# Gated attention in float32: probabilities transposed on TensorE, or turned in 32x32 blocks on VectorE and moved by DMA

## The chip, the cores and the metric

The kernel runs on one core of one Trainium2 chip. Times are device microseconds of an execution. A profiled execution has its own span, from its first to its last instruction, which is a little shorter than the time that is measured around an execution. The engines are named as in the profile: PE is TensorE (its weight loads apart as PEld), DVE is VectorE, ACT is ScalarE, POOL is GpSimd, and SP is SyncE, whose queue issues all DMAs here.

## The reference, cut to what matters

```python
# x: (4, 512, 256); 16 query heads of 128, 4 key heads
xn = layernorm(x)
Q = (xn @ Wq + bq).reshape(b, l, 16, 128)
K, V = the same with Wk, Wv for 4 heads; head h uses key head h % 4
scores = einsum('blhe,bmhe->bhlm', Q, K) / sqrt(128)
attn = softmax(scores + causal_mask)
ctx = einsum('bhlm,bmhe->blhe', attn, V).reshape(b, l, 2048)
r = xn + gelu(ctx @ Wo + bo)
s = layernorm(r) * gamma + beta
g = silu(swiglu_ffn(xn))          # inner size 1024
return x + s * g
```

All of it is float32. The kernel keeps that accuracy on TensorE by splitting each operand into two parts, hi[...] and lo (the exact rest); `product` (L93) issues three matmuls, hi*hi, hi*lo and lo*hi, on L95, L96 and L97.

## The kernel before, in words

The program has two phases. In the first (up to L589) the tokens of each of the four batches are normed, transposed and put through the feed-forward gate; what the second phase needs of them is written to DRAM (`xT_dram`, `fin_dram`). The second phase is the attention.

The attention works in **groups** (b, g): a batch and a key head with its four query heads. A group has four **steps**, i = 0 to 3, one for each tile of 128 queries; the list `steps` (L560) holds all 64, and the last group goes through its steps in reverse. A step sees i+1 tiles of 128 keys. In the main loop (L632 to L662) each step gives a list of chunks with positions, which are sorted and issued in that order; the framework then schedules the instructions of each engine from that order of priority and the dependences.

For step s the loop issues:

- `scores` (L415) of the next step, in four sub-tiles t of 32 queries of each of the four heads, so that the rows of a sub-tile are (head, query). TensorE makes the scores in a PSUM bank `ps` (two banks); VectorE reduces them with the mask and takes the row minimum (L449); ScalarE does exp with the row sum in `total` (L460); VectorE takes the reciprocal of one column of `total` (L473); GpSimd scales the row (L474). The result stays in one of two tiles `p`, one for each parity of the step's number.
- `transposed_probs` (L476) for each key tile j of step s: four transposes on TensorE against the identity (L481) into a PSUM bank `pt`, which bring (head, query) of the four sub-tiles to columns; then `split_psum` (L82) makes hi on ScalarE (L86) and lo on VectorE (L87). The pairs `pT` live in four slots with the tag "pt".
- `weighted` (L486): pT against the values, accumulated over j in `pc`; at the end `ctxT` is split off it (L89, L90).
- `projected` (L503) of step s-1 with the weights `wos[g]`, and what later steps need: `ahead` (L602) issues `queries` (L401) of the next group, `keys` and `values`.
- now and then the end of the batch before: `activated`, `load_fin`, `finished` (L524 to L544), and the reload of the next batch's transposed tokens (`reload`, L235).

The weights of the projections, `wqs[g]` and `wos[g]`, are loaded and split once by `load_group` (L553) in batch 0 and stay in SBUF for all batches. They take eight of the ten slots of 8 KB per partition with the tag "w"; the other two hold the weights of keys and values.

Of the kernel before, what the change touches and what calls it, by code (L numbers as in the profile page):

```python
# [17 lines left out]
P = 128  # L18
EPS = 1e-5
S = 32  # queries of a head in a tile of scores  # L20
MASK = -1e9
HIGHEST = 3.4028235e38
# [4 lines left out]
def kernel(  # L27
    ctx: ExitStack,
    tc: tile.TileContext,
    x: bass.AP,  # [B, L, D]  # L30
    wq: bass.AP,  # [D, H*E]
    bqT: bass.AP,  # [E, H]
    wk: bass.AP,  # [D, KV*E]
    bkT: bass.AP,  # [E, KV]
    wv: bass.AP,  # [D, KV*E]
    bvT: bass.AP,  # [E, KV]
    wo: bass.AP,  # [H*E, D]
    bo: bass.AP,  # [D]
    gamma: bass.AP,  # [D]
    beta: bass.AP,  # [D]  # L40
    wguT: bass.AP,  # [D, 2*INTER]
    wdT: bass.AP,  # [INTER, D]
    out: bass.AP,  # [B, L, D]
):
# [37 lines left out]
    def split_psum(dst, src, bias=None):  # L82
        """dst[:, 0] = hi, dst[:, 1] = lo of a bank of PSUM (plus a bias per partition)."""
        hi, lo = dst[:, 0], dst[:, 1]
        if bias is None:
            first = nc.scalar.copy(hi, src)  # L86
            second = nc.vector.tensor_tensor(lo, src, hi.bitcast(F32), ALU.subtract)  # L87
        else:
            first = nc.scalar.activation(hi, src, AF.Identity, bias=bias)  # L89
            second = nc.vector.scalar_tensor_tensor(lo, src, bias, hi.bitcast(F32), ALU.add, ALU.subtract)  # L90
        return first, second

    def product(out_ap, lhs, rhs, first, last, **kw):  # L93
        """out += lhs^T rhs; lhs and rhs are (hi, lo)."""
# [19 lines left out]
    def load_w(name, views, hi_on=None, lo_on=None):  # L114
        """A slot of 1024 columns of weights, in two parts."""
# [17 lines left out]
    # Probabilities of a query tile: [32 queries of each head of a group, sub-tile of 32  # L133
    # queries, keys], the last key that the tile sees in the last column. What a sub-tile
    # doesn't see of the last P keys stays zero.
    p_tiles = [const.tile([P, NT, L], F32, name=f"p{k}") for k in range(2)]

# [18 lines left out]
    # The first tokens and the first weights come in small pieces, in the order of their use.  # L156
# [14 lines left out]
    def split_first(f, lo_on=None):  # L171
        """The columns of f of the first slot of the gate's weights."""
# [8 lines left out]
    # Keeps the tensor engine busy until the first tokens are there, so that its clock is up by then.  # L181
# [114 lines left out]
    ff_tags = [("s", 2), ("s", 2), ("t", 2), ("t", 2), ("mm", 1), ("c", 1)]  # L296
    def h_tiles(b):
        """Places for the eight tiles of a batch among those of the attention phase."""
# [4 lines left out]
        else:  # L303
            yield from (pair("k", 4, f"hk_{b}_{k}") for k in range(4))
        if b % 2:
            yield from (pair("v", 5, f"hv_{b}_{k}") for k in range(4))
# [57 lines left out]
    banks = ["mm", "c"]  # "c" only until the first values are weighted  # L364
# [5 lines left out]
    def whole(dst, t):  # L370
        """The first P columns as they were before they were split: so few columns go
        faster through the tensor engine whole."""
        nc.gpsimd.tensor_tensor(dst, t[:, 0].bitcast(F32), t[:, 1].bitcast(F32), ALU.add)  # L373

    def keys(b, g):
# [4 lines left out]
        k = pair("k", 4, f"kT_{b}_{g}")  # L380
# [20 lines left out]
    def queries(b, g, r):  # L401
        h = r * KV + g
        pq = psum.tile([P, L], F32, tag=free_bank(), bufs=1, name=f"pq_{b}_{h}")
        w = wqs[g]
# [3 lines left out]
        if r == 0:  # L408
            # [E, part, sub-tile of S queries, head of g, query]
# [6 lines left out]
    def scores(b, g, i, t):  # L416
        """Causal scores of sub-tile t of query tile i, of the four heads of g, as
        probabilities. Kept negated up to exp, so that the minimum of a row is the bias
        that exp wants."""
# [53 lines left out]
        latest["dve"] = [nc.vector.reciprocal(total[:, r : r + 1], total[:, r : r + 1])]  # L473
        latest["pool"] = [nc.gpsimd.tensor_scalar(pr, pr, total[:, r : r + 1], 1.0, ALU.mult, ALU.mult)]  # L474
# [11 lines left out]
    def weighted(b, g, i, j):  # L486
        """Transposed probabilities against the values: [E, heads of g, queries of i]."""
# [17 lines left out]
    def projected(b, g, i, r):  # L505
        first = g == 0 and r == 0 and i < 2
        if first:
# [6 lines left out]
            (wos[g][:, 0, ts(r, D)], wos[g][:, 1, ts(r, D)]),  # L514
# [19 lines left out]
    def finished(b, t, last):  # L534
        """Residual, second layer norm, gate and the outer residual of token tile t."""
# [23 lines left out]
    load_group(0)  # L559
# [8 lines left out]
    for b in range(B):  # L568
        for f in range(NI):
# [14 lines left out]
            elif f == 6:  # L584
                values(0, 0)
            else:
                keys(0, 1)
    for t in range(NT):
        down(B - 1, t)  # L589
    for p in p_tiles:  # L590
        clear(p, L)
    for r in range(G):
        scores(0, 0, 0, r)
        if r > 1:
            keys(0, r)
    values(0, 1)
    banks = ["mm"]
    load_group(1)

    # ---- attention: scores run one step ahead of the weighted values, queries one  # L600
    # group, the projection one step behind ----
    def ahead(b, g, n):  # L602
        """What later steps need."""
        if g == 0 and n + 1 < NT and (b, n) != (0, 0):
            yield values, (b, n + 1)
        dist = TUNE.get("qd", (1, 1, 1, 1))
        mine = range(sum(dist[:n]), sum(dist[: n + 1]))
        if g + 1 < KV:
            for r in mine:
                yield queries, (b, g + 1, r)  # L610
        elif b + 1 < B:
            if n == 0:
                reload(b + 1)
            yield keys, (b + 1, n)
            for r in mine:
                yield queries, (b + 1, 0, r)
            if n == NT - 1:
                yield values, (b + 1, 0)

    def load_group_behind(g, half):  # L620
        with behind("pool"):
            load_group(g, half)
# [9 lines left out]
    for s, (b, g, i) in enumerate(steps[:-2]):  # L632
        n = s % NT
        chunks = []
        for m, (f, a) in enumerate(ahead(b, g, n)):
            # The scores of the next group follow its last queries.
            pos = TUNE.get("a0", 0.01) + TUNE.get("a1", 0.3) * m
            chunks.append((min(pos, -1.0) if f is queries and n == NT - 1 else pos, f, a))
        for r in range(G):
            if s + 4 < len(steps):  # L640
                chunks.append((TUNE.get("s0", 0.05) + TUNE.get("s1", 0.17) * r, scores, steps[s + 1] + (r,)))
            elif s + 4 == len(steps):
                for m in range(1, 4):
                    chunks.append((TUNE.get("l0", 0.05) + TUNE.get("l1", 0.17) * r + TUNE.get("l2", 0.1) * m, scores, steps[s + m] + (r,)))
# [14 lines left out]
        if b == 0 and g + 2 < KV and n in (1, 2):  # L659
            chunks.append((0.9, load_group_behind, (g + 2, n - 1)))  # L660
# [3 lines left out]
    # The last two steps run side by side.  # L664
# [84 lines left out]
```

## Time and profile before

| | |
|---|---|
| time, median of 3 runs (lowest, highest) | 681.08 us (680.22, 681.22) |
| span of the profiled execution | 679.5 us |
| mean granted TensorE clock | 0.994 |
| DMA, mean over the span | 51 GB/s; SP's queue 15.4% of 16 engines |
| bytes moved | 34.73 MB |
| L474, scaling on POOL | x256, mean 505 ns, 127.6 us busy |
| L460, exp on ACT | x256, mean 522 ns, 133.2 us busy |
| L87, lo of pT on DVE | x160, mean 686 ns, 106.6 us busy |
| L86, hi of pT on ACT | x160, mean 587 ns, 89.2 us busy |
| L473, reciprocal on DVE | x256, mean 158 ns, 38.4 us busy |

The span and every duration are those of one profiled execution. "Busy" is the time in which an engine had an instruction in work; matmuls overlap in their pipeline, so that the durations of single matmuls add up to more than TensorE's time. A row of the group table names the line, the engine, the operation, what it writes and reads, the shape, the count, the busy time with the mean of one in ns, and the idle time of the engine just before with what ended it. The chain of waits goes back from the last instruction to whatever released it.

### The profile page before, as it was taken

How to read it: one execution, taken by the hardware profiler on the slowest of the kernel's cores; microseconds unless marked ns; L12 is line 12 of the kernel's file. 1: busy time of each engine (PE TensorE's matmuls, PEld its weight loads, DVE VectorE, ACT ScalarE, POOL GpSimd, SP SyncE). 2: the span in 40 equal slices, each digit the busy share in tenths (PEclk: the TensorE clock that was granted, in tenths of full speed). 3: DMA queues.
4: the chain of work that ended last, by engine and by line, in shares of the span. 5: the costliest groups of instructions: out<-in, count | busy, mean ns of one | idle time of the engine just before them, and what ended most of it. 6: DMA issues, size and time to landing. Idle time of an engine off the chain costs nothing.

```text
span 679.5 us, 12006 instructions
## 1 busy us (share of the span) xinstructions
PE 661.7 (97%) x3996; PEld 581.6 (86%) x3996; DVE 447.8 (66%) x1337; ACT 402.6 (59%) x956; POOL 273.4 (40%) x490
## 2 busy tenths in 40 slices
PE   7979999999999999999999999999999999999995
PEld 6768888889889888888888898889888988888984
DVE  5864434165766766775787666668867766687867
ACT  4434333253765766677676665957666668576772
POOL 5588130720646423222353232216433323354332
PEclk8999999999999999999999999999999999999998
DMA  7753322211310100000022000002210000032000
GB/s 223 246 191 122 127 81 90 77 47 50 92 31 2 36 29 1 1 0 1 20 76 94 1 0 1 2 1 63 63 62 1 1 2 1 1 93 79 1 1 32
DMA packets 25262, 34.73 MB, mean 51 GB/s; under 512 B 2288, under 2 KB 18544, under 8 KB 25200
## 3 DMA queue, kind: packets, MB, share of 16 engines
q1 hardware_dynamic: 25200, 33.97, 15.4%
q8 instruction: 31, 0.51, 0.3%
q14 instruction: 31, 0.25, 0.1%
HBM read 21.38 MB, written 12.58 MB: 50 GB/s over the span
## 4 chain that ended last, share of the span: by engine, by line
PE 89%; DVE 4%; DMA 4%; issue 1%; ACT 1%; POOL 1%; SPq 0%; ACTq 0%; DVEq 0%; POOLq 0%
PE pt L481 10%; PE pc L96 5%; PE pc L95 5%; PE pc L97 5%; PE pq L95 5%; PE py L97 4%; PE ps L97 4%; PE ps L96 4%; PE pq L97 4%; PE pq L96 4%; PE py L95 4%; PE ps L95 4%; PE py L96 4%; PE pg L97 3%; PE pg L96 3%; PE pg L95 3%
## 5 line engine op out<-in xcount | busy, mean ns | idle before, releaser
L474 POOL TENSOR_SCALAR p<-p,total 128x320 f32<-128x320 f32 (+15 forms) x256 | 127.6, 505 | 195.5 <-DVE total L473 174.9
L460 ACT ACTIVATE p<-p,least 128x320 f32<-128x320 f32 (+15 forms) x256 | 133.2, 522 | 59.7 <-DVE least L449 51.0
L449 DVE CUSTOM_DVE_ANT_0 p<-ps,mask 128x320 f32<-128x320 f32 (+15 forms) x256 | 109.8, 435 | 42.6 <-PE ps L97 17.5
L86 ACT CAST pT<-pt 128x512 fp32r<-128x512 f32 x160 | 89.2, 587 | 60.0 <-PE pt L481 59.2
L87 DVE TENSOR_TENSOR pT<-pt,pT 128x512 fp32r<-128x512 f32 x160 | 106.6, 686 | 25.5 <-ACT pT L86 25.0
L481 PE MATMUL pt<-ident,p 128*128 128x128 f32 x640 | 107.2, 273 | 0.5 <-POOL p L474 0.5
L481 PEld LDWEIGHTS pt<-ident,p 128*128 128x128 f32 x640 | 81.1, 142 | 17.5 <-POOL p L474 0.7
L97 PE MATMUL py<-w_o,ctxT 128*128 128x256 f32 x256 | 73.5, 287 | 0.6 <-DVE ctxT L90 0.6
L95 PE MATMUL py<-w_o,ctxT 128*128 128x256 f32 x256 | 72.9, 285 | 0.1
L96 PE MATMUL py<-w_o,ctxT 128*128 128x256 f32 x256 | 72.1, 281 | 0.0
L96 PE MATMUL pc<-pT,v 128*128 128x512 f32 x160 | 69.1, 432 | 0.0
L95 PE MATMUL ps<-kT,qT 128*128 128x288 f32 (+3 forms) x192 | 68.5, 357 | 0.0
L373 POOL TENSOR_TENSOR q<-qT 128x128 f32<-128x128 f32 x64 | 30.4, 474 | 93.7 <-DVE qT L90 55.8
L95 PE MATMUL pc<-pT,v 128*128 128x512 f32 x160 | 64.5, 403 | 0.1
L97 PE MATMUL pc<-pT,v 128*128 128x512 f32 x160 | 63.2, 395 | 0.0
L473 DVE RECIPROCAL total<-total 128x1 f32<-128x1 f32 x256 | 38.4, 158 | 37.2 <-ACT p L460 35.1
L96 PE MATMUL ps<-kT,qT 128*128 128x288 f32 (+3 forms) x192 | 62.2, 324 | 0.0
L97 PE MATMUL ps<-kT,qT 128*128 128x288 f32 (+3 forms) x192 | 61.7, 322 | 0.0
L90 DVE SCALAR_TENSOR_TENSOR qT<-pq,bq_sb,qT 128x512 fp32r<-128x512 f32 x64 | 47.9, 748 | 15.3 <-ACT qT L89 15.3
L89 ACT ACTIVATE qT<-pq,bq_sb 128x512 fp32r<-128x512 f32 x64 | 44.0, 687 | 20.1 <-PE pq L97 19.6
L90 DVE SCALAR_TENSOR_TENSOR ctxT<-pc,bv_sb,ctxT 128x512 fp32r<-128x512 f32 x64 | 47.8, 747 | 11.1 <-ACT ctxT L89 10.5
L95 PE MATMUL pg<-xT,w_gu 128*128 128x512 f32 (+1 forms) x132 | 50.5, 397 | 3.9 <-DVE h L338 2.5
(127 smaller groups left out, 1567.5 us busy)
## 6 DMA issues: line engine op xcount, KB each, us to landing
fin<-fin_dram SPq DMA_DIRECT2D x16, 384.0 KB, 3.2
xT_dram<-xT SPq DMA_DIRECT2D x8, 512.0 KB, 2.6
fin_dram<-gate SPq DMA_DIRECT2D x16, 256.0 KB, 2.0
xT_again<-xT_dram SPq DMA_DIRECT2D x8, 512.0 KB, 3.9
fin_dram<-xn SPq DMA_DIRECT2D x16, 128.0 KB, 2.4
st_q<-in_wq_dram SPq DMA_DIRECT2D x8, 256.0 KB, 3.2
st_o<-in_wo_dram SPq DMA_DIRECT2D x4, 512.0 KB, 3.9
out_dram<-y SPq DMA_DIRECT2D x16, 128.0 KB, 1.7
```

Source lines behind the costliest of these rows:

```text
L86: first = nc.scalar.copy(hi, src)
L87: second = nc.vector.tensor_tensor(lo, src, hi.bitcast(F32), ALU.subtract)
L89: first = nc.scalar.activation(hi, src, AF.Identity, bias=bias)
L90: second = nc.vector.scalar_tensor_tensor(lo, src, bias, hi.bitcast(F32), ALU.add, ALU.subtract)
L95: nc.tensor.matmul(out_ap, lhs[0], rhs[0], start=first, stop=False, **kw)
L96: nc.tensor.matmul(out_ap, lhs[0], rhs[1], start=False, stop=False, **kw)
L97: nc.tensor.matmul(out_ap, lhs[1], rhs[0], start=False, stop=last, **kw)
L449: nc.vector.tensor_tensor_reduce(pr, ps[:, :seen], mask[:, L - seen :], scale=-SCALE, scalar=HIGHEST, op0=ALU.add, op1=ALU.min, accum_out= ...
L460: exp = nc.scalar.activation(pr, pr, AF.Exp, bias=least[:, r : r + 1], scale=-1.0, accum_out=total[:, r : r + 1],)
L473: latest["dve"] = [nc.vector.reciprocal(total[:, r : r + 1], total[:, r : r + 1])]
L474: latest["pool"] = [nc.gpsimd.tensor_scalar(pr, pr, total[:, r : r + 1], 1.0, ALU.mult, ALU.mult)]
L481: nc.tensor.transpose(pt[:, :, t], p[:, t, ts(j, P)], ident)
```

## The change

For the steps that `moved` names (i > 0, and not one of the last three), the probabilities no longer go through TensorE to be transposed:

- The reciprocal is taken once for a step, of all four columns of `total`, behind the fourth exp. The four scalings on GpSimd follow it (`normalized`).
- VectorE turns each scaled sub-tile in blocks of 32x32 (`nc.vector.transpose`) into a tile `pu` in a "w" slot.
- `exchanged` writes `pu` to DRAM in one DMA, and reads it back in four DMAs, each of which lands in 32 partitions, into `pw` in another "w" slot. The blocks are then where the transposes would have put them.
- `transposed_probs` splits `pw`: hi on ScalarE, lo on VectorE for even j and on GpSimd for odd j, both from SBUF.

Scores run three steps ahead (`AHEAD`). Steps i = 0 have two tiles of their own for the probabilities (`p_first`), and are transposed on TensorE as before. Because `pu` and `pw` use "w" slots, the weights of the projections don't stay: their split form is written to DRAM in batch 0 (`w_dram`) and loaded for each later group. Keys are made two groups ahead in three slots in place of four; queries of the next groups, the reload of xT and the loads of weights move to other steps.

```diff
+AHEAD = 3
...
+    p_first = [const.tile([P, NT, P], F32, name=f"pf{k}") for k in range(2)]
...
+    w_dram = {(k, g): dram.tile([P, 2, 1024], F32, tag=f"w{k}{g}", name=f"w_dram_{k}{g}") for k in "qo" for g in range(KV)}
...
-        k = pair("k", 4, f"kT_{b}_{g}")
+        k = pair("k", 3, f"kT_{b}_{g}")
...
+            elif i == 0:
+                p = p_first[(b * KV + g) % 2]
             else:
                 p = p_tiles[steps.index((b, g, i)) % 2][:, :, L - n :]
...
-        latest["dve"] = [nc.vector.reciprocal(total[:, r : r + 1], total[:, r : r + 1])]
-        latest["pool"] = [nc.gpsimd.tensor_scalar(pr, pr, total[:, r : r + 1], 1.0, ALU.mult, ALU.mult)]
+        if t == G - 1:
+            latest["dve"] = [nc.vector.reciprocal(total, total)]
+            for k in range(NT):
+                normalized(b, g, i, k)
+
+    def normalized(b, g, i, t):
+        p, _, total = probs[b, g, i]
+        pr = p[:, t, : i * P + (t + 1) * S]
+        latest["pool"] = [nc.gpsimd.tensor_scalar(pr, pr, total[:, t : t + 1], 1.0, ALU.mult, ALU.mult)]
+        if moved(b, g, i):
+            if t == 0:
+                turned[b, g, i] = work.tile([P, NT, i + 1, NT, S], F32, tag="w", bufs=10, name=f"pu_{b}_{g}_{i}")
+            u = turned[b, g, i]
+            nc.vector.transpose(u[:, :, :, t], p[:, t].rearrange("p (j c k) -> p c j k", c=NT, k=S))
+
+    def moved(b, g, i):
+        return i > 0 and (b, g, i) not in steps[-3:]
+
+    def exchanged(b, g, i):
+        u = turned.pop((b, g, i)).rearrange("p c j t n -> p (c j t n)")
+        n = (i + 1) * P
+        d = dram.tile([G, S, NT, n], F32, tag="pd", bufs=3, name=f"pd_{b}_{g}_{i}")
+        nc.sync.dma_start(d.rearrange("r k c n -> (r k) (c n)"), u)
+        w = work.tile([P, G, n], F32, tag="w", bufs=10, name=f"pw_{b}_{g}_{i}")
+        for c in range(NT):
+            nc.sync.dma_start(w[ts(c, S)], d[:, :, c].rearrange("r k n -> k r n"))
+        placed[b, g, i] = w
 
     def transposed_probs(b, g, i, j):
+        if moved(b, g, i):
+            src = placed[b, g, i][:, :, ts(j, P)]
+            t = pair("pt", 4, f"pT_{b}_{g}_{i}_{j}")
+            hi, lo = (t[:, k].rearrange("p (r n) -> p r n", r=G) for k in range(2))
+            nc.scalar.copy(hi, src)
+            (nc.gpsimd if j % 2 else nc.vector).tensor_tensor(lo, src, hi.bitcast(F32), ALU.subtract)
+            pT[b, g, i, j] = t
+            return
...
-    def load_group(g, half=None):
-        if half != 1:
-            wqs[g] = load_w(f"q{g}", [wq_v[c, g] for c in range(ND)])
-        if half != 0:
-            wos[g] = load_w(f"o{g}", [wo_v[g]])
+    def load_group(kind, ph):
+        b, g = divmod(ph, KV)
+        to = wqs if kind == "q" else wos
+        if b == 0:
+            views = [wq_v[c, g] for c in range(ND)] if kind == "q" else [wo_v[g]]
+            to[ph] = load_w(f"{kind}{g}", views)
+            nc.sync.dma_start(w_dram[kind, g], to[ph].bitcast(F32))
+        else:
+            to[ph] = work.tile([P, 2, 1024], F32R, tag="w", bufs=10, name=f"w_{kind}_{b}_{g}")
+            nc.sync.dma_start(to[ph].bitcast(F32), w_dram[kind, g])
...
+    for i in range(1, AHEAD):
+        for r in range(G):
+            scores(0, 0, i, r)
+            if i == AHEAD - 1 and r % 2:
+                queries(0, 1, r // 2)
+        exchanged(0, 0, i)
...
+        ph = b * KV + g
+        if n == NT - 1:
+            if ph + 2 < B * KV:
+                yield keys, divmod(ph + 2, KV)
+                for r in range(2):
+                    yield queries, (*divmod(ph + 2, KV), r)
+        if n == 0 and ph + 1 < B * KV:
+            for r in range(2, G):
+                yield queries, (*divmod(ph + 1, KV), r)
...
+        if s + AHEAD < len(steps):
+            step = steps[s + AHEAD]
+            for r in range(G):
+                chunks.append((TUNE["s0"] + TUNE["s1"] * r, scores, step + (r,)))
+            if moved(*step):
+                chunks.append((1.9, exchanged, step))
...
+        if n == 1 and ph + 1 < B * KV:
+            chunks.append((0.9, load_group_behind, ("o", ph + 1)))
+        if n == 0 and ph + 2 < B * KV:
+            chunks.append((0.9, load_group_behind, ("q", ph + 2)))
+        if n == 1 and g == KV - 2 and b + 1 < B:
+            chunks.append((0.9, reload, (b + 1,)))
```

More of the change, by code (lines that the diff above doesn't have):

```diff
@@ L303, in h_tiles @@
         else:
-            yield from (pair("k", 4, f"hk_{b}_{k}") for k in range(4))
+            yield from (pair("k", 3, f"hk_{b}_{k}") for k in range(3))
         if b % 2:
-            yield from (pair("v", 5, f"hv_{b}_{k}") for k in range(4))
+            yield from (pair("v", 5, f"hv_{b}_{k}") for k in range(5))
     n_ff = 0
@@ L403, in queries @@
         pq = psum.tile([P, L], F32, tag=free_bank(), bufs=1, name=f"pq_{b}_{h}")
-        w = wqs[g]
+        w = wqs[b * KV + g]
         for c in range(ND):
@@ L513, in projected @@
             (c[:, 0, ts(r, P)], c[:, 1, ts(r, P)]),
-            (wos[g][:, 0, ts(r, D)], wos[g][:, 1, ts(r, D)]),
+            (wos[b * KV + g][:, 0, ts(r, D)], wos[b * KV + g][:, 1, ts(r, D)]),
             first,
@@ L551 @@
     wv_sb = load_w("v", [wv.rearrange("(c p) n -> p c n", p=P)])
-    def load_group(g, half=None):
-        if half != 1:
-            wqs[g] = load_w(f"q{g}", [wq_v[c, g] for c in range(ND)])
-        if half != 0:
-            wos[g] = load_w(f"o{g}", [wo_v[g]])
-    load_group(0)
+    def load_group(kind, ph):
[8 more added lines that the diff above has]
+            nc.sync.dma_start(to[ph].bitcast(F32), w_dram[kind, g])
+    load_group("q", 0)
+    load_group("o", 0)
     steps = []
@@ L587 @@
                 keys(0, 1)
+    placed, turned = {}, {}
     for t in range(NT):
@@ L591 @@
         clear(p, L)
+    for p in p_first:
+        clear(p, P)
+    load_group("q", 1)
     for r in range(G):
         scores(0, 0, 0, r)
-        if r > 1:
-            keys(0, r)
     values(0, 1)
     banks = ["mm"]
-    load_group(1)
+    for i in range(1, AHEAD):
[4 more added lines that the diff above has]
+        exchanged(0, 0, i)
     def ahead(b, g, n):
@@ L605, in ahead, with load_group_behind @@
             yield values, (b, n + 1)
[L606 to L622, printed above, removed]
+        ph = b * KV + g
[7 more added lines that the diff above has]
+                yield queries, (*divmod(ph + 1, KV), r)
+        if g == KV - 1 and b + 1 < B and n == NT - 1:
+            yield values, (b + 1, 0)
+    def load_group_behind(kind, ph):
+        with behind("pool") if ph < KV else nullcontext():
+            load_group(kind, ph)
     def finished_behind(b, t):
@@ L637 @@
             pos = TUNE.get("a0", 0.01) + TUNE.get("a1", 0.3) * m
[L638 to L644, printed above, removed]
+            chunks.append((pos, f, a))
+        if s + AHEAD < len(steps):
[4 more added lines that the diff above has]
+                chunks.append((1.9, exchanged, step))
         for j in range(i + 1):
@@ L658 @@
                 chunks.append((TUNE.get("fin_pos", 0.7), finished_behind, (b - 1, n)))
-        if b == 0 and g + 2 < KV and n in (1, 2):
-            chunks.append((0.9, load_group_behind, (g + 2, n - 1)))
+        ph = b * KV + g
+        if n == 1 and ph + 1 < B * KV:
[4 more added lines that the diff above has]
+            chunks.append((0.9, reload, (b + 1,)))
         for _, f, a in sorted(chunks, key=lambda c: c[0]):
```

## The prediction

> **What bounds the kernel now.** I read the busy table and the chain of waits first, then windows of one batch, then the rows of the operations that the change touches.
>
> ```profile
> PE 661.7 (97%) x3996; PEld 581.6 (86%) x3996; DVE 447.8 (66%) x1337; ACT 402.6 (59%) x956; POOL 273.4 (40%) x490
> ...
> PE pt L481 10%; PE pc L96 5%; PE pc L95 5%; PE pc L97 5%; PE pq L95 5%; PE py L97 4%; PE ps L97 4%; PE ps L96 4%; PE pq L97 4%; PE pq L96 4%; PE py L95 4%; PE ps L95 4%; PE py L96 4%; PE pg L97 3%; PE pg L96 3%; PE pg L95 3%
> ...
> L481 PE MATMUL pt<-ident,p 128*128 128x128 f32 x640 | 107.2, 273 | 0.5 <-POOL p L474 0.5
> ```
>
> TensorE is busy 97% of the span, and nearly every link of the chain is a TensorE product that waits for nothing. The transposes of L481 are the chain's largest line. Their row overstates them: 273 ns is a pipelined duration. The chain in order of time, in one stretch, has the real price:
>
> ```profile
> 307.57 0.19 PE ps L97
> 307.76 0.44 PE pt L481 x4
> 308.20 0.24 PE pq L95
> 308.44 0.23 PE pq L96
> ```
>
> Four transposes hold TensorE for 0.44 us, so one costs 0.11 us (and a product of 512 columns 0.23 us). Next, the batch between two reloads of xT, then the early stretch in which the DMA engines were saturated:
>
> ```profile
> 363.44:493.00 129.56, 129.16 (x796) 114.14 (x795) 91.77 (x298) 87.44 (x213) 46.18 (x92) 1.00 0.08 26
> ```
> ```profile
> 44.00:48.00 4.00, 4.00 (x21) 3.34 (x20) 0.69 (x1) 0.61 (x2) 1.64 (x2) 1.00 1.04 349
> ```
>
> After the length come busy us of TensorE, its weight loads, VectorE, ScalarE and GpSimd, then granted clock, DMA share and GB/s. A batch has 4 groups (b, g), so a group takes 32.4 us, with VectorE busy 22.9, ScalarE 21.9 and GpSimd 11.5; DMA is nearly idle (0.08). The second line gives the DMA ceiling: about 349 GB/s.
>
> **TensorE: what goes.** A group has steps i = 0 to 3, step i with i+1 key tiles of four transposes. Steps i > 0 hold 4 x (2+3+4) = 36. All 16 groups: 576, less the last three steps' 12+8 = 20: 556. At 0.11 us: **61.2 us** off the path, 4.0 us a group, leaving 28.4. (The chain's 10% of 679.5 us, times 556/640, says 59.) No matmul is added.
>
> **The engines that take over.** VectorE gains twelve 32x32 transposes a group. No row shows one. Nearest are its passes over as many elements: L449 takes 0.55 us for 384 columns and 0.68 for 512; by these 4 x (0.42+0.55+0.68) = 6.6 us; at twice that,[...] 13.2; below 6.6 nothing in the trace points. I take 6.6. One reciprocal replaces four: 12 x 0.158 = 1.9 less. Nine differences from PSUM at 0.686 = 6.2 go; five from SBUF come back. L343, two SBUF inputs, takes 0.74 to 1.05 us, and 0.68 is the lowest such row (L112 on VectorE): 3.4 to 5.2. Sum 24.8 to 26.6 of 28.4. GpSimd gets the other four differences: L112 there takes 1.35 us, 5.4 more: 17 of 28.4. ScalarE's copies read SBUF (L342, 0.62) in place of PSUM (0.587): 22.2. None of the three exceeds 28.4; with the dear transposes VectorE would need 31 to 33, about the present pace.
>
> **DMA.** Per group each moved step writes and reads 512, 768 or 1024 KB: 2.36 MB each way. The weights no longer stay in place (two loads of 1 MB a group; in batch 0 a write of 1 MB beside each of wq and wo's own first load, 3.1 MB). Reloads of xT, fin and out are 0.8 MB as before. Sum 7.6 MB, at 349 GB/s **21.8 us of 28.4**: it fits, but the queue goes from 8% to three quarters full.
>
> **The wait that is added.** A step's probabilities now make a round trip: scores, exp, scaling, turning, write, read, split, weighted product. Landing times:
>
> ```profile
> xT_dram<-xT SPq DMA_DIRECT2D x8, 512.0 KB, 2.6
> fin_dram<-gate SPq DMA_DIRECT2D x16, 256.0 KB, 2.0
> xT_again<-xT_dram SPq DMA_DIRECT2D x8, 512.0 KB, 3.9
> ...
> out_dram<-y SPq DMA_DIRECT2D x16, 128.0 KB, 1.7
> ```
>
> 128, 256 and 512 KB written land after 1.7, 2.0 and 2.6 us: 1.4 us plus 0.3 per 128 KB. The write takes 2.6, 3.2 and 3.8 us for i = 1, 2, 3. Reads: the reload's shortest landing is 3.2 us for 512 KB, which leaves about 2.0 fixed. By these rows a read takes 3.2, 3.8 and 4.4 us.
>
> [...] Each exchange reads in four DMAs that land in 32 partitions each (32c to 32c+31); every large transfer of this trace spans 128.[...] The data part then doubles: 4.4, 5.6 and 6.8 us. By the row the queue holds 21.8 us a group[...]. No row of before decides it[...].
>
> Before the write, the tail of a step of 512 columns shows the chain up to the scaling:
>
> ```profile
> 317.47 0.40 PE L97 MATMUL ps<-kT,qT 128*128 128x512 f32 x1
> 318.02 0.69 DVE L449 CUSTOM_DVE_ANT_0 p<-ps,mask 128x512 f32<-128x512 f32 x1 [0.66 <-PE pt L481]
> 318.89 0.73 ACT L460 ACTIVATE p<-p,least 128x512 f32<-128x512 f32 x1
> 319.74 0.16 DVE L473 RECIPROCAL total<-total 128x1 f32<-128x1 f32 x1
> 320.07 0.70 POOL L474 TENSOR_SCALAR p<-p,total 128x512 f32<-128x512 f32 x1 [2.01 <-DVE total L473]
> ```
>
> From the product's end (317.87) to the start of scaling (320.07) is 2.2 us. Now one reciprocal serves four sub-tiles, so four scalings start together: 0.62+0.67+0.70+0.70 = 2.7, then the last transpose 0.7: 5.6 us. Write 3.8, SP's issue 0.35 (0.34 per DMA in the queue's timeline), read 6.8, copy 0.62 and difference 0.68 to 1.35 (1.0): **18.2 us for i = 3 with nothing in the way**; 15.8 by the row. For i = 2: 4.9+3.2+0.35+5.6+1.6 = 15.7 (13.9).
>
> Against this stands TensorE's work between the last score of a step and its first weighted product in the changed program's order, counted at the rates above: medians of 16.2 us for i = 1, 14.3 for i = 2, 16.9 for i = 3. That is all the cover "three ahead" gives. What is in the way: SP is in order, each read waits there for its write to land, and the next write, weights, fin and out stand behind it. In most groups the 1 MB load of wq stands before the write of i = 3: 1.05 MB/349 = 3.0 us. Engine queues add about 0.5 (the 448-column pair before the tail above took 3.8 us where the tail took 2.9). So i = 3 needs 18.2+3.5 = 21.7 against 16.9, a stall of **4.8 us a group**; i = 2 needs 15.7+1.0 = 16.7 against 14.3, which mostly falls into the same stall; I add 0.5. Break-even is 4.0.
>
> **Sum against the profiled execution.** 15.4 groups (556/36): 679.5 - 61.2 + 15.4 x 5.3 = 699.9 us; with the 1.6 us by which the median (681.08) exceeds the span: **702 us**, 3% slower. Edits at nothing: GpSimd's two clears of p_first and the three smaller reciprocals of i = 0 (GpSimd is 60% idle; uncovered under 1 us); loads of weights moved a group later (wq stands half a group before its first query; if late, 3 us once a group, as in the upper rival). The first phase, some 170 us, and the last three steps are unchanged.
>
> **Rivals.** (1) *Faster: reads run as the reload's row.* Then i = 3 needs 15.8+3.0 = 18.8, a stall of 1.9: 679.5-61.2+29.3+1.6 = **649**. For it: the only reads in the trace, and DMA at 8%. Against: the landing shape. It decides wherever the stall stays under 4.0 us a group. (2) *Much slower: the late landing feeds itself.* In the new VectorE order the difference of step 1 (it waits for its read) stands before the transposes of step 3, and that of step 3 before the next group's. So VectorE closes a loop: exchange 1 (2.6+0.35+4.4 = 7.4), difference 0.7, two reductions, exp, scaling, turning 5.5, exchange 3 (11.0), difference 0.7, the next group's 4: 29.3, and with wq ahead 32.3 before any other queueing. Behind a waiting difference also stand the reductions that empty the two score banks, so TensorE stops in one piece.[...] this trace shows 1.00 in every stretch of the attention, 0.91 only in its first 20 us. By the row such stalls cost their length[...]. With both: stalls of 8 us, 679.5-61.2+123+1.6 = **743**.[...] (3) *Even:* gain and stalls cancel, 4.0 each, **681**. That the change doesn't do what it says: the new order has 84 transposes left of 640, so no.
>
> **Chances.** 702: 0.40; 649: 0.32; 743: 0.20; 681: 0.08. The likeliest's own range is 686 to 722 (queueing of 2.5 to 4.8). Range **640 to 755**. A difference of 0.2% is what this measurement can tell: faster 0.35 (rival 1 and 0.03 of the even case), same 0.04, slower 0.61.
>
> **What would show it.** Right: L481 with 84 instructions; TensorE's idle grown to about 80 us, before weighted products whose differences wait for pw; DMA share near 0.7 in the attention; the read's landing clearly above 4.4 us for i = 3. Wrong: landings of 4.4 or less with TensorE busy over 95% (rival 1); granted clock under 1.00 in mid-attention (rival 2); transposes at 1.3 us for 512 columns would make VectorE the bound.

## The result, and the profile after

The changed kernel takes **765.92 us** at the median (764.16 to 773.1, 4 runs) against 681.15 us before (680.22 to 682.73): a ratio of 1.126, 95% interval 1.1226 to 1.1294. The direction of the forecast holds; its size does not, 85 us slower in place of 21. The profiled execution is one of 773.1 us with a span of 771.0, 91.5 us above the span of before, and all accounts below are of such single executions.

From the profile of the changed kernel: busy times, the chain by engine, five rows of the group table (line, engine, operation, what it writes and reads, count, busy us and mean ns, then the idle time ahead of it and what ended it), and DMA issues (KB each, median us to landing).

```profile
PE 659.5 (86%) x3440; PEld 552.7 (72%) x3440; DVE 499.0 (65%) x1267; ACT 397.4 (52%) x956; POOL 359.7 (47%) x558
...
PE 35%; DMA 32%; DVE 14%; ACT 7%; SPq 5%; issue 4%; POOL 2%; ACTq 0%; DVEq 0%; POOLq 0%
...
L520 POOL TENSOR_TENSOR pT<-pw,pT 128x512 fp32r<-128x512 f32 x62 | 84.4, 1368 | 167.7 <-ACT pT L519 153.3
...
L519 ACT CAST pT<-pw 128x512 fp32r<-128x512 f32 x139 | 77.7, 615 | 104.4 <-DMA pw<-pd 101.0
...
L520 DVE TENSOR_TENSOR pT<-pw,pT 128x512 fp32r<-128x512 f32 x77 | 74.1, 965 | 70.4 <-ACT pT L519 70.4
L96 PE MATMUL pc<-pT,v 128*128 128x512 f32 x160 | 73.3, 458 | 48.8 <-ACT pT L519 48.1
...
L495 DVE STREAM_TRANSPOSE pu<-p 128x256 f32<-128x256 f32 (+2 forms) x184 | 94.9, 555 | 2.1 <-POOL p L488 1.9
...
pd<-pu SPq DMA_DIRECT2D x16, 1024.0 KB, 6.8
pw<-pd SPq DMA_DIRECT2D x64, 256.0 KB, 5.3
...
pw<-pd SPq DMA_DIRECT2D x60, 192.0 KB, 3.9
...
pw<-pd SPq DMA_DIRECT2D x60, 128.0 KB, 2.8
```

556 matmuls are gone (3996 to 3440), but TensorE's busy time fell by 2 us only. So the remaining ones became slower, and on top TensorE is idle for 111 us of the span where it was idle for 18. The chain, nearly all TensorE before, is one third DMA. The wait runs down a line of engines: the read ends ScalarE's idle time (L519, 101.0 us), and ScalarE's hi part (the cast to fp32r) ends that of VectorE and GpSimd (L520) and TensorE's ahead of weighted products (48.1 us), which begin with hi. The batch between two reloads of xT took 129.6 us before; it is now

```profile
395.17:541.40 146.23, 124.73 (x646) 104.14 (x646) 103.54 (x270) 84.18 (x208) 67.31 (x106) 0.94 0.63 200
```

with a granted clock of 0.94 in place of 1.00 and a DMA share of 0.63 in place of 0.08 (columns as in the forecast). The clock is the first thing that the forecast's sum did not have.

To see what the pieces are worth I added up TensorE's time from the last product of the first phase to the end, counting for each matmul the time from its start to the next one's start (its own duration at most), and the gaps between as idle:

| us, one execution each | span | transposes | idle | all other products |
|---|---|---|---|---|
| before | 679.5 | 54.4 | 2.3 | 447.8 |
| after | 771.0 | 7.7 | 95.6 | 491.3 |
| difference | +91.5 | -46.7 | +93.3 | +43.5 |

The three differences sum to 90.1; the first phase and the tail bring 1.4. Most of the 43.5 us is work at half clock: between the first and the last product of the attention the trace grants half speed for 85.3 us, against none before. TensorE stands idle for 16 of these. In the other 69 a product of 512 columns starts 0.43 us after the one before at the median, against 0.23 at full clock; this and the granted 0.50 put the loss at 34 us, an estimate. The remaining 9.5 us lie at full clock, in products just ahead of a gap: the sum counts a product of 512 columns there with its own 0.4 us, where the next would have started after 0.23. They belong to the waits.

Two stretches of the after trace, each a window of 3.41 us and the next one (length, then busy us of TensorE, its weight loads, VectorE, ScalarE and GpSimd, then granted clock, DMA share, GB/s):

```profile
369.49:372.90 3.41, 1.89 (x11) 1.45 (x10) 1.89 (x8) 1.79 (x4) 0.58 (x1) 1.00 1.07 378
372.90:376.31 3.41, 3.41 (x10) 2.44 (x9) 3.25 (x10) 1.55 (x7) 1.86 (x3) 0.50 0.96 380
```
```profile
441.19:444.60 3.41, 0.33 (x3) 0.30 (x2) 1.99 (x8) 2.61 (x7) 1.39 (x2) 1.00 1.00 411
444.60:448.01 3.41, 3.41 (x11) 2.77 (x10) 1.31 (x4) 0.37 (x2) 1.99 (x5) 0.50 0.32 130
```

In each pair TensorE is idle for a part of the first window and then works through the second at half speed, 10 and 11 products where the full-speed window from 448.01 holds 21. In the first pair 1.52 us of idle came ahead of the half clock.

### The profile page after: what moved, and what is told of

It reads as the page before. It is cut to its first block, busy times and chain, and to the rows that moved or that the text cites. A ratio compares the mean times of both kernels' runs of the same rounds, so it can differ in the third digit from the quotient of the medians.

```text
span 771.0 us, 11159 instructions
## 1 busy us (share of the span) xinstructions
PE 659.5 (86%) x3440; PEld 552.7 (72%) x3440; DVE 499.0 (65%) x1267; ACT 397.4 (52%) x956; POOL 359.7 (47%) x558
## 4 chain that ended last, share of the span: by engine, by line
PE 35%; DMA 32%; DVE 14%; ACT 7%; SPq 5%; issue 4%; POOL 2%; ACTq 0%; DVEq 0%; POOLq 0%
DMA pw<-pd 18%; DMA pd<-pu 13%; DVE pu L495 5%; SPq L511 5%; PE pg L97 4%; PE pg L96 4%; PE pg L98 4%; ACT pT L519 3%; PE pc L96 3%; PE pc L97 2%; PE pd L96 2%; PE pc L98 2%; PE pd L98 2%; PE pd L97 2%; DVE p L456 2%
## 5 line engine op out<-in xcount | busy, mean ns | idle before, releaser
L520 POOL TENSOR_TENSOR pT<-pw,pT 128x512 fp32r<-128x512 f32 x62 | 84.4, 1368 | 167.7 <-ACT pT L519 153.3
L467 ACT ACTIVATE p<-p,least 128x160 f32<-128x160 f32 (+3 forms) x196 | 111.1, 568 | 45.7 <-DVE least L456 37.7
L519 ACT CAST pT<-pw 128x512 fp32r<-128x512 f32 x139 | 77.7, 615 | 104.4 <-DMA pw<-pd 101.0
L488 POOL TENSOR_SCALAR p<-p,total 128x160 f32<-128x160 f32 (+3 forms) x196 | 105.4, 559 | 43.7 <-DVE total L481 35.8
L520 DVE TENSOR_TENSOR pT<-pw,pT 128x512 fp32r<-128x512 f32 x77 | 74.1, 965 | 70.4 <-ACT pT L519 70.4
L96 PE MATMUL pc<-pT,v 128*128 128x512 f32 x160 | 73.3, 458 | 48.8 <-ACT pT L519 48.1
L456 DVE CUSTOM_DVE_ANT_0 p<-ps,mask 128x160 f32<-128x160 f32 (+3 forms) x196 | 94.0, 487 | 28.9 <-PE ps L98 27.8
L495 DVE STREAM_TRANSPOSE pu<-p 128x256 f32<-128x256 f32 (+2 forms) x184 | 94.9, 555 | 2.1 <-POOL p L488 1.9
L97 PE MATMUL pc<-pT,v 128*128 128x512 f32 x160 | 71.1, 444 | 5.4 <-POOL pT L520 3.5
L96 PE MATMUL ps<-kT,qT 128*128 128x160 f32 (+2 forms) x192 | 66.2, 345 | 2.1 <-DVE least L456 1.8
L96 PE MATMUL pq<-xT_again,w_q 128*128 128x512 f32 x128 | 56.1, 438 | 12.6 <-DVE qT L91 7.8
L97 PE MATMUL ps<-kT,qT 128*128 128x160 f32 (+2 forms) x192 | 64.1, 334 | 0.0
L98 PE MATMUL ps<-kT,qT 128*128 128x160 f32 (+2 forms) x192 | 63.8, 332 | 0.0
L96 PEld LDWEIGHTS py<-w_o,ctxT 128*128 128x128 f32 x256 | 49.4, 193 | 17.8 <-ACT ctxT L90 15.0
```

What stands on the lines that cost most here:

```text
L96: nc.tensor.matmul(out_ap, lhs[0], rhs[0], start=first, stop=False, **kw)
L97: nc.tensor.matmul(out_ap, lhs[0], rhs[1], start=False, stop=False, **kw)
L98: nc.tensor.matmul(out_ap, lhs[1], rhs[0], start=False, stop=last, **kw)
L456: nc.vector.tensor_tensor_reduce(pr, ps[:, :seen], mask[:, L - seen :], scale=-SCALE, scalar=HIGHEST, op0=ALU.add, op1=ALU.min, accum_out= ...
L467: exp = nc.scalar.activation(pr, pr, AF.Exp, bias=least[:, r : r + 1], scale=-1.0, accum_out=total[:, r : r + 1],)
L488: latest["pool"] = [nc.gpsimd.tensor_scalar(pr, pr, total[:, t : t + 1], 1.0, ALU.mult, ALU.mult)]
```

## The experiments

All ratios are against the kernel before on the same chip, with their 95% intervals. "Exchange" means the DMA write and its four reads; "turning" the 32x32 transposes on VectorE.

**What does the exchange cost, what VectorE's load, what the rearrangement?** Three kernels take the change apart. In the first the splits take `pu` itself, so that no block changes its partitions; in the second GpSimd's scaling writes `pu` as well, and VectorE turns nothing; the third moves no step, keeps the three steps of lookahead and the reloaded weights, and gives the probabilities "w" slots of their own.

```diff
 def exchanged(b, g, i):                       # e1, e5
-    nc.sync.dma_start(d..., u)
-    for c in range(NT): nc.sync.dma_start(w[ts(c, S)], d[:, :, c]...)
+    w = u.rearrange("p (r n) -> p r n", n=n)
 def normalized(b, g, i, t):                   # e5
-    tensor_scalar(pr, pr, ...); nc.vector.transpose(u[:, :, :, t], ...)
+    nc.gpsimd.tensor_scalar(flat[:, t], p[:, t], ...)
 def moved(b, g, i):                           # e8
-    return i > 0 and (b, g, i) not in steps[-3:]
+    return False
```

> The write to DRAM and the reads back are left out: the splits take the turned blocks as they lie in SBUF, so blocks stand in the wrong places of the output; all else stays, the reloaded weights too. If the loss sits in the round trip through DRAM (its landing times and what waits behind them), TensorE is the bound again: 620 to 645 us, clock 0.99. If the added work on VectorE, GpSimd and ScalarE or the reloaded weights cost it, 690 us or more remain.

> As the run without the exchange (680 us), and the turning is left out too: GpSimd's scaling writes the tile that the splits read, over all columns, so blocks stand unturned. VectorE loses 184 instructions, some 95 us of work. If VectorE's load is what ate the gain in the run without the exchange, the time falls to 635 to 655 us. If it is GpSimd, ScalarE, the reloaded weights or the new order of queries and keys, it stays at 670 to 685.

> No step is moved: all probabilities go through TensorE as before, in tiles of their own; scores still run three steps ahead, weights are still written to DRAM and reloaded, reciprocals are merged, queries and keys stand where the change put them. If the rearrangement and the reloaded weights are harmless, 680 to 688 us; if they cost by themselves, 695 us or more.

Measured: e1 679.8 us, 0.9983 [0.9963, 1.0003]; e5 648.76 us, 0.9521 [0.9505, 0.9537]; e8 682.67 us, 1.0015 [1.0006, 1.0024]. So the rearrangement costs nearly nothing, and with turning and exchange both gone the removed transposes bring 34 us. The turning takes 31 us of that back although it issues nothing on TensorE. The exchange costs the other 86 us. The surprise was e1: I had expected 620 to 645 us. The window 360 to 480 us, first of e1, then of e5:

```profile
360.00:480.00 120.00, 113.48 (x632) 97.13 (x631) 104.68 (x268) 83.13 (x203) 68.20 (x105) 1.00 0.26 93
```
```profile
360.00:480.00 120.00, 115.05 (x650) 99.62 (x649) 83.75 (x233) 86.30 (x212) 71.53 (x109) 1.00 0.27 97
```

In e1 VectorE is busy 104.68 of 120 us, 87%, in e5 70%, with the clock at 1.00 in both windows. An engine at 87% is not full, and yet TensorE loses: by the sum above its idle time is 38.2 us in e1 and 20.3 in e5, and over the whole attention e1 runs 13.7 us at half clock, e5 none. The longest such wait, VectorE's queue in e1 first, then TensorE's:

```profile
208.17 4.22 DVE L516 TENSOR_TENSOR pT<-pu,pT 128x512 fp32r<-128x512 f32 x1
...
212.89 0.74 DVE L91 SCALAR_TENSOR_TENSOR ctxT<-pc,bv_sb,ctxT 128x512 fp32r<-128x512 f32 x1
```
```profile
213.68 0.39 PE L98 MATMUL py<-w_o,ctxT 128*128 128x256 f32 x1 [3.92 <-DVE ctxT L91]
```

The instruction that TensorE waits for stands behind a difference that took 4.22 us, where the mean of its line in e1 is 1.15, and behind one reduction. Waits for this line sum to 10.1 us in e1 and 2.6 in e5. Such long differences are not the turning's own: e5 has one of 4.28 us at the same place, and TensorE waits 1.49 us there. That the turning makes VectorE's queue longer is seen; how its 31 us divide among the waits was not followed further.

**Is the exchange's cost the wait as such, or its volume?** e12 keeps every write and its four reads, but of 64 columns.

```diff
-        d = dram.tile([G, S, NT, n], F32, tag="pd", ...)
-        nc.sync.dma_start(d.rearrange("r k c n -> (r k) (c n)"), u)
+        d = dram.tile([P, 64], F32, tag="pd", ...)
+        nc.sync.dma_start(d, u[:, :64])
         for c in range(NT):
-            nc.sync.dma_start(w[ts(c, S)], d[:, :, c].rearrange("r k n -> k r n"))
+            nc.sync.dma_start(u[ts(c, S), :64], d[ts(c, S)])
```

> The changed kernel with each exchange kept as a round trip, but of 64 of the columns only (32 KB written, four reads of 8 KB back into the same tile); the splits take the tile. Left out: the move of the blocks between partitions. Without an exchange the kernel took 680 us, with the full one 766 us. If what the exchange costs is the volume (transfers of 0.5 to 1 MB at some 200 to 400 GB/s, and what they put in each other's way), a small round trip of about 4 us is nearly covered: 680 to 700 us. If it is that any wait for a DMA in the order of the engines stalls TensorE, most of the 86 us stays: 735 us or more. Between them, the share of each is read off: at 710 us, 30 us belong to the wait itself and 56 us to the volume.

Measured: 679.34 us, 0.9968 [0.995, 0.9986], the same as with no exchange. ScalarE's row of e12, and two rows of its DMA issues:

```profile
L519 ACT CAST pT<-pu 128x512 fp32r<-128x512 f32 x139 | 79.0, 616 | 14.2 <-DMA pu<-pd 10.7
```
```profile
pu<-pd SPq DMA_DIRECT2D x184, 8.0 KB, 1.6
...
pd<-pu SPq DMA_DIRECT2D x46, 32.0 KB, 1.5
```

A round trip of 1.5 + 1.6 us is covered (10.7 us of waiting, not 101.0). The 86 us go with the volume, 0.5 to 1 MB each way, and with what waits behind such transfers. e1, e5 and e12 also take no slot for `pw`; but in the changed kernel the turning does not wait for a slot there (2.1 us of idle ahead of L495, ended by the scaling), and SP's queue shows no wait of note for one.

**Does VectorE's load still count when the exchange is there?** e11 is e5's scaling with the full exchange.

> The changed kernel with the exchange as it is, but without the turning on VectorE: GpSimd's scaling writes the tile that is written to DRAM. Left out: the transposition inside the 32x32 blocks. Without the exchange, the turning cost 31 us (680 against 649 us). If load and exchange add up, this kernel takes about 735 us. If the wait for the round trip hides VectorE's load, since turning adds only 0.7 us to a trip of 24 us, it takes 755 to 766 us. If VectorE's load lengthens every trip by queueing, it gains more than 31 us: under 725 us.

Measured: 740.07 us, 1.0831 [1.0773, 1.0889]. Against 766 us the turning costs 26 us here by the medians, 29 by the ratios, and 31 us without an exchange: the two costs nearly add.

**What makes the volume so dear: the shape in which the reads land, the order of VectorE's queue, the load of wq?** e2 reads into all 128 partitions in each of the four DMAs. e4 issues the splits of a step only behind the next moved step's last turning, scaling and exp, so that no waiting split stands ahead of them. e13 is both, e10 is e4 with the 1 MB load of wq behind the reads of i = 3.

```diff
-            nc.sync.dma_start(w[ts(c, S)], d[:, :, c].rearrange("r k n -> k r n"))    # e2, e13
+            nc.sync.dma_start(w[:, c], d[:, :, c].rearrange("r k n -> (r k) n"))
...
+            with ExitStack() as stack:                                                 # e4, e10, e13
+                for ins in last.get(steps[nxt], []):
+                    stack.enter_context(tc.issue_after(ins.ins))
                 nc.scalar.copy(hi, src)
```

> The four reads of a step each land in 128 partitions with n columns in place of 32 partitions with 4n: same bytes, same packet length, same count, but the heads and key blocks are not exchanged, so the output is not the reference's. [...] the read of 1 MB gets some 2.4 us shorter and the time falls to 690 to 725 us. If reads are bound by packets or by DRAM, landings stay (5.3 us at 1 MB) and the time stays at 755 to 775.

> The splits of a moved step are queued behind the next moved step's turning (VectorE), scaling (GpSimd) and last exp (ScalarE), so that no engine holds the next exchange back while it waits for a landing. Nothing else changes. If the late landing feeds itself through VectorE's and GpSimd's order, the loop opens: 695 to 735 us. If each step's own round trip is longer than its cover, the order is no matter: 755 to 775 us.

> e2_reads_128 and e4_order in one: reads into 128 partitions (750 us alone) and the splits queued behind the next exchanged step's turning and exp (738 us alone); the changed kernel is at 766 us. Left out: the blocks land in the wrong partitions. If the two add up, 722 us. If both shorten the same wait in the loop of exchange and VectorE's order, the second is worth less: 730 to 738 us. If the shorter reads, with the loop cut, bring the trip under the cover, it falls below 710 us.

> As e4_order (738 us), with the 1 MB load of wq queued behind the four reads of i = 3 in place of ahead of their write. In the changed kernel the 1 MB write landed after 6.8 us at the median, against 3.8 us in e7_only_i3. If the load of wq is what lies in the way (3.0 us a group in the forecast's sum, 12 groups), the write lands near 4 us and the time falls by 20 to 36 us: 702 to 718 us. If it is the saturated reads of i = 2 and the engines' order that delay the trip, the time stays within 10 us of 738.

Measured: e2 749.56 us, 1.099 [1.0946, 1.1034]; e4 738.2 us, 1.0843 [1.0799, 1.0887]; e13 730.2 us, 1.0719 [1.0686, 1.0752]; e10 739.66 us, 1.0827 [1.0785, 1.0868]. The landing shape is worth 16 us alone, the order 28, both 36: they shorten partly the same wait. Moving the load of wq gains nothing. With it behind the reads the 1 MB write lands after 4.3 us, not 6.3 as in e4, but TensorE then waits 7.4 us for wq ahead of queries, 3.0 in e4.

The shape in the trace of after: a stretch in which reads into 32 partitions fill the queue, ahead of a load of wo, and one with a write and a load of wq, both over 128 partitions (same columns as above):

```profile
451.00:452.00 1.00, 1.00 (x10) 1.00 (x9) 0.05 (x1) 0.69 (x1) 0.00 (x0) 1.00 1.02 223
```
```profile
442.00:443.00 1.00, 0.00 (x0) 0.00 (x0) 0.36 (x1) 1.00 (x2) 0.00 (x0) 1.00 1.03 426
```

At the same full share of the DMA engines the first moves 223 GB/s and the second 426. In e2 a read of 256 KB lands after 4.1 us in place of 5.3.

The loop that e4 cuts stands in the chain of waits of after, in order of time (start, us, what):

```profile
422.39 5.39 DMA pd<-pu
...
429.11 2.81 DMA pw<-pd
...
431.95 0.05 DVEq L520
432.00 0.53 DVE pu L495
432.53 0.02 issue
432.54 3.25 DMA pd<-pu
...
437.11 4.71 DMA pw<-pd
...
442.51 1.13 ACT pT L519 x2
```

The read that lands at 431.92 releases a difference (L520) in VectorE's queue, behind which the turning of the next step (432.00) had to stand, and with it the next write. Two exchanges that don't depend on each other run one after the other.

**Fewer exchanges.** e7 moves only i = 3, e14 only i = 1, e15 i = 1 and i = 2; the other steps are transposed on TensorE as in e8. e7 and e15 carry e4's lines as well, but these act only where the step named there is moved: in e7 nowhere, in e15 for i = 1.

```diff
-        return i > 0 and (b, g, i) not in steps[-3:]
+        return i == NT - 1 and (b, g, i) not in steps[-3:]     # e7; e14: i == 1; e15: 0 < i < 3
```

> Only the steps with four key tiles are moved (15 of them), with the splits in the order behind the next moved step; the others go through TensorE. TensorE saves 240 transposes, 26 us; VectorE's turning, GpSimd's splits and the exchanges' bytes fall to less than half (1 MB each way of 2.4 MB a group). If the load of VectorE and the chained exchanges made the loss, 665 to 685 us, about the kernel before; if one late exchange a group is enough to stall TensorE, 700 us or more.

> Only steps i = 1 exchanged (512 KB each, 15 of them), the others transposed on TensorE as in e8_none_moved (683 us). 120 transposes go, 13 us. Its trip is the shortest: about 4.5 us to the end of turning, 3.2 us of write, 0.35 us of issue, 2.5 to 2.8 us of reads, 1.5 us of splits, 12 us, against some 14 to 16 us of TensorE work; VectorE gains only four short turnings a group. If volume is the cost, this one is covered: 668 to 676 us, faster than the kernel before. If even a single covered exchange stalls TensorE through the queues of VectorE and ScalarE, the time is at or above 683 us.

> Steps i = 1 and i = 2 exchanged, i = 3 transposed on TensorE; the splits queued behind the next exchanged step's turning as in e4_order. 300 transposes go, 33 us. If the long transfers of i = 3 and what stands in their way are the bulk of the cost, 665 to 685 us. If VectorE's load and the two trips' coupling are enough to stall TensorE, 695 to 720 us.

Measured: e7 725.32 us, 1.0641 [1.0586, 1.0695]; e14 684.75 us, 1.0051 [1.0032, 1.007]; e15 720.55 us, 1.0581 [1.054, 1.0621]. One 1 MB exchange a group is enough to stall: e7 is 43 us above e8. This is a trip in e7's timeline, with little in its way (start, us, engine, line; in brackets the wait; L510, L513 and L526 are the changed kernel's L508, L511 and L519):

```profile
390.96 0.40 PE L98 MATMUL ps<-kT,qT 128*128 128x512 f32 x1
...
397.34 0.71 DVE L495 STREAM_TRANSPOSE pu<-p 128x512 f32<-128x512 f32 x1
...
398.07 0.32 SPq L510 DMA_DIRECT2D pd<-pu  x1
403.02 1.74 SPq L513 DMA_DIRECT2D pw<-pd  x4
...
411.23 0.50 PE L96 MATMUL pc<-pT,v 128*128 128x512 f32 x1 [2.32 <-ACT pT L526]
```

From the last score's end (391.36) to the first weighted product it takes 19.9 us: 6.7 to the write, 5.0 for the write, 8.2 for reads and split. Over all 16 trips the median is 19.8 us to the start of the hi part and 21.1 to the end of the first difference, against a median of 17.8 us that TensorE works ahead of the first weighted product. e14 is the mildest form, and still no gain: 120 transposes fewer are worth 9.6 us by the sum above, but idle time grows from 4.7 us (e8) to 13.8.

**More cover, or a busy TensorE.** e6 is e4 with four steps of lookahead, e9 is e7 with four; both make all four queries of a head two groups ahead. e3 puts six products that nobody reads ahead of the first weighted product of each moved step, to keep the clock up.

```diff
-AHEAD = 3
+AHEAD = 4                                                    # e6, e9
...
+            for _ in range(6):                               # e3
+                nc.tensor.matmul(idle, c[:, 0, :P], c[:, 0], start=True, stop=True)
```

> With the splits queued behind the next turning (738 us so far), scores run four steps ahead, with one more buffer for the row sums and the DRAM tile, and all four queries of a head two groups ahead. If cover is what lacks, a step more (some 7 us of TensorE work) takes away most waits of TensorE for its splits and gives 695 to 720 us. If slots, the SP queue or VectorE bind, 730 to 750 us.

> Only steps i = 3 exchanged, as in e7_only_i3 (725 us), with scores four steps ahead in place of three (and all four queries of a group made at its step n = 3). In e7 the trip of an i = 3 step took about 19 us with little in its way, against some 10 to 12 us of TensorE work between its last score and its first weighted product. If the stall is only too little cover, a fourth step ahead adds about 7 us of cover, the stall of about 8 us a group nearly goes, and the time falls by 50 to 100 us less the rest of the load on the other engines: 650 to 685 us. If more lookahead again only moves the wait to slots of the tag w and to late weights, as in e6_ahead4, the time stays at 715 to 760 us.

> Six extra products of 512 columns, which nobody reads, stand before the first weighted product of each moved step: 1.4 us of TensorE work at full clock, 44 x 1.4 = 62 us in all, in the place where TensorE waits. If the halved clock after the waits is a cost of its own, the mean clock goes from 0.943 to above 0.97 and the time falls by 10 to 35 us (730 to 755) although work is added. If the clock only follows the waits and costs little, the time grows by 5 to 40 us.

Measured: e6 758.84 us, 1.1149 [1.1107, 1.1191], e9 744.36 us, 1.0894 [1.0856, 1.0931], e3 777.5 us, 1.1401 [1.1377, 1.1426]. A fourth step made both slower. In e9 it added no cover: the work that TensorE does between the last score of i = 3 and its first weighted product stayed at a median of 17.5 us (e7 17.8). So the "10 to 12 us" of cover in e9's expectation was wrong too. Why e9 is 19 us slower than e7 was not followed up. In e6 TensorE's wait for the hi part fell from 28.8 us (e4) to 15.8, but that for reloaded wq rose from 3.0 to 11.2, and others with it. In e3 idle fell from 95.6 to 59.7 us and the half clock from 85.3 to 47.8 us, but the fill itself is 62 us of work.

## Why the forecast was wrong, step by step

- **"One costs 0.11 us", 61.2 us saved.** Over the whole trace of before, 640 transposes hold TensorE for 54.4 us, 0.085 each, and the change saved 46.7. I took one link of the chain of waits, where a piece starts only when the chain reaches it. The timeline of the same place in the kernel before says

```profile
307.60 0.60 PE L481 MATMUL pt<-ident,p 128*128 128x128 f32 x4
307.95 0.48 PE L95 MATMUL pq<-xT_again,w_q 128*128 128x512 f32 x1
```

  so four take 0.35 us from their start to the next product's. The term was 14.5 us too large.

- **The clock at 1.00 in the sum.** This is the largest miss: 34 us. A lower clock stood in the forecast only with the second rival; that waits bring it on was not shown by the trace of before. In the runs about 1.5 us of idle in a window of 3.41 were enough (below).

- **"None of the three exceeds 28.4", so the engines that take over cost nothing.** This is the step that failed in kind. I compared VectorE's busy sum (24.8 to 26.6 us) with the group's 28.4 us and read 90% busy as hidden. e1 against e5 puts 31 us on the turning alone, e11 against the changed kernel 26 to 29. The work itself was sized right: 0.421, 0.555 and 0.679 us for turning 256, 384 and 512 columns, against 0.42, 0.55 and 0.68 in the forecast.

- **"15.4 x 5.3" = 81.6 us of stalls.** Idle grew by 93.3. Of the 95.6 us, 38.2 stand in e1 without any exchange, so the exchange's own part is 57.4. The term came out near the whole because it was too large for what it named and left out the other. That 5.3 us a group is near the measured stall (a median of 6.0 us of idle between the last score of i = 3 and its first weighted product, over all causes) is luck. The trip takes 27.0 us at the median to the end of the first difference, not 21.7, and 21.1 in e7, not the 18.2 "with nothing in the way"; and TensorE works 20.2 us under it, in part at half clock, not 16.9.

- **The reads into 32 partitions.** The forecast doubled the data part of the reads, an assumption of mine that no row of before showed. The rates measured since agree with it: 223 GB/s at full share in place of 426, the latter also above the 349 that the forecast took for the ceiling. The forecast by the row would have missed it. But its 6.8 us for the reads of i = 3 were worth only 16 us of the end time (e2), so this choice did not decide between faster and slower: e2 is still 10% slower than before.

- **The second rival's loop, and "SP is in order".** The loop through VectorE's order exists (the chain above; 28 us in e4), and I gave it 0.20 as an alternative, though nothing in the profile excluded it beside the likeliest case. Its sign, a granted clock under 1.00 in mid-attention, came together with those of the likeliest case. Whether wq's load costs its 3.0 us stays open: moving it only moved the wait (e10).

- **Edits at nothing.** Rearrangement, reloaded weights and clears: e8 is 0.15% above before. Right.

So of the 71.1 us between the forecast's 699.9 and the span of 771.0, the clock is 34.0, the transposes 14.5, the idle time 11.7 net of two opposite errors, the part of the waits that hides in the products' own durations 9.5, and the first phase and the tail 1.4.

What stays open: e13 leaves 50 of the exchange's 86 us unexplained in parts. That they go with the volume is shown (e12); whether by the landing times alone or by transfers in each other's way was not separated. SP's queue, which issues every DMA, stood for 179 us in the changed kernel until writes had landed (45 waits ahead of the reads; between the write at 441.24 and its reads at 447.70 it issued nothing); no version issues from a second queue. Nor was it separated why 20 us of idle remain in e5. No version that does the whole work was faster than the kernel before.

## What to carry to other kernels

When work is moved off a bound engine, ask of the engine that takes it not only whether its sum fits, but who waits for which instruction in its queue: here 87% busy already cost nearly what the move had saved (31 of 34 us). A transfer that waits is only as cheap as its length against the work between its two ends, counted in the final schedule (21.1 us against 17.8 in e7), and a difference that waits for it must not stand ahead of what starts the next transfer. Price what is saved by the time to the next instruction's start, summed over the trace, and price stalls with the slower clock that followed them here (34 us).

## What the runs showed of the hardware

The clock fell after waits well short of a window. The granted clock changes on a grid of 3.41 us (at half speed in the attention of after: stretches of 3.41, 6.83 and 17.07 us). In all seventeen profiled executions of this study I set TensorE's idle time in each full-speed window of the attention beside the clock of the next: 130 windows were followed by half clock, 124 of them with at least 1.5 us idle; 2,368 were not, none with more than 1.81. Between 1.5 and 1.81 us both occur. In after alone 15 windows were followed by half clock, with 1.52 to 3.09 us idle; the others had 1.65 at most. So about half a window of idle was enough, in one piece or in several (one such window of after has 2.06 us of idle, no piece of it over 1.19). Stalls of 2 us, as in this kernel, already paid for it.

GpSimd's difference of two SBUF tiles takes 1.37 us at the mean and VectorE's 0.97, where the forecast had 1.35 and 0.68 to 1.05. VectorE's mean mixes two cases: 0.69 us where GpSimd has no instruction in the time (6 of 77 in after) or one for at most 30% of it (28 of 77), and 1.18 where it has one for over 30% (43 of 77). So VectorE's difference took half a microsecond more at the mean beside GpSimd's work; which of GpSimd's instructions do it was not tested.
